# Input weights loaded in one piece per gate, and the weight sums of the head shared out anew (GRU with residual, one core)

## The chip, the cores and the metric

The kernel runs on one core of a Trainium2 chip. The metric is the device time of one execution in microseconds (us). Engines are named as in the profile: PE is TensorE (PEld its weight loads), DVE is VectorE, ACT is ScalarE, POOL is GpSimd, SP is SyncE, which here only issues DMAs.

## The reference

A GRU with 64 sequences, 128 steps and 512 features, all fp32; the output is the input plus the new state of every step. After each fourth step, except the last, the state goes through one more layer ("prop").

```python
comb  = concat([x_t, h])
z     = sigmoid(comb @ Wz + bz)
r     = sigmoid(comb @ Wr + br)
cand  = tanh(concat([x_t, r * h]) @ Wh + bh)
h_new = (1 - z) * h + z * cand
h     = tanh(h_new @ Wp + bp) if (t + 1) % 4 == 0 and t < T - 1 else h_new
out[:, t] = x_t + h_new
```

Wz, Wr and Wh have 1024 rows: the upper 512 meet x_t, the lower 512 meet the state.

## The kernel before

**Layout.** A tile has 128 partitions in four quarters of 32. The batch is split into two halves of 32 sequences, h = 0 and 1, and features into four blocks of 128. A half's rows stand on partitions by feature block. The state has to be turned for the products (features on partitions): VectorE does this in 32 x 32 blocks (`turn`, L238, for the state; `join_x`, L251, for x). Gates are called R, Z and H_ in the code; H is the candidate's gate.

**Two kinds of products.** The *hidden* part of each gate (state times the lower weights `wh`, and `wp` for prop) is the recurrence: `gate` (L218) adds it into the PSUM banks `rec[0]`, `rec[1]` (gates R, H and prop of half 0 and half 1) and `rec_z`. The *input* part (x times the upper weights `wx`) doesn't depend on the state, and is worked out ahead of need. For steps 0 to 3 it is done plainly (`plain`, L413); VectorE adds the bias and writes a tile `cp` (`add_bias`, L417). From step 4 on it is done in batches of four steps (`batch`) with a scheme of seven products in place of eight, on two levels, after Strassen and Winograd. It needs sums and differences of weights, made once in the head: on the outer level `tw` (six of 128 x 768, `sum_outer`, L286) and `d5` (two of 128 x 768, `sum_outer_1`, L292), on the inner level `tt` and `din` (`sum_inner` and `sum_inner_1`, L296 to L302: for each of seven operands i four of 128 x 384; operand 5 needs d5, operands 4, 6 and 7 need tw). It also needs sums of the turned x (`four`, L306; `sum_raw12`, `sum_raw34`, `sum_s12` and so on), which GpSimd makes. GpSimd also adds the bias (`with_bias`, L549) and puts the products together into `cp` (`add`, L544; `pair_left` and `pair_right` for the first batch of steps 4 to 7).

**Seeds.** Ahead of a gate, ScalarE copies the input part with bias from `cp` into the PSUM bank (`seed`, L376 to L379), and TensorE adds the hidden part onto it. Each engine takes its instructions in the order in which the program writes them. A gate in a bank `rec[h]` waits for every earlier write to this bank, also where the seed is for another gate's half of it.

**The order of a step.** `half(h)` (L781) is a generator that runs all steps of one half of the batch; two of them are interleaved, the second 700 columns behind the first. A step is gate R, gate Z, gate H, and prop after each fourth step; between them `fill` takes input products from a queue, as many as the tables PLACES, HEAD and TAIL say. Second half only: `behind_r`, `join` and `behind_step` write the GpSimd sums, the turns of x and the DMAs of the step. Seeds of step t+1 are written as soon as a bank is free; gate R's seed of step 4 is written in step 3, behind gate Z (L818 to L820), since `cp` of step 4 is late.

**The head.** Loads: x of steps 0 and 1 (`xr`), then the input weights of R, Z and H, with `load_w` (L98), each in four DMAs of 32 partitions (R in two halves of four), two of them on SyncE's queue and two on ScalarE's. Feature q\*128 + 32k + e of x lies on partition 32q + e in block k of `wx`, and join_x turns x to match. GpSimd's own DMA queue brings the biases and the first state. Then `later_loads` (L144): hidden weights, further x, Wp and the bias of prop. In the program stand next: two turns of x of steps 0 and 1, `later_loads`, the turn of the first state, the sums for operands 1 and 2 on VectorE, d5 and the sums for 3 and 5 on GpSimd, the plain products of steps 0 and 1 on TensorE with cp behind them, the seeds of step 0, and the steps.

Of the kernel before, what the change touches and what calls it, by code (L numbers as in the profile page):

```python
# [9 lines left out]
F32 = mybir.dt.float32  # L10
# [8 lines left out]
def kernel(  # L19
# [14 lines left out]
    nc = tc.nc  # L34
# [3 lines left out]
    S = 2  # L38
# [52 lines left out]
    def load_x(tile_, t0, n, j=0, engs=(nc.sync, nc.sync)):  # L91
        for h in range(S):
            for q in (0, 2, 1, 3):
                engs[q // 2].dma_start(
                    out=tile_[part(q), j : j + n, h, :], in_=x[ts(h, V), t0 : t0 + n, ts(q, J)]
                )

    def load_w(wt, w, k0=0, k1=K, engs=(nc.sync, nc.sync)):  # L98
        for q in (0, 2, 1, 3):
            engs[q // 2].dma_start(  # L100
                out=wt[part(q), k0:k1, :],
                in_=w[q * P + k0 * V : q * P + k1 * V, :].rearrange("(k e) n -> e k n", e=V),
            )

    both_queues = (nc.sync, nc.scalar)

    xr = {}
# [7 lines left out]
    new_xr(0)  # L115
    load_x(xr[0], 0, 2, engs=both_queues)
    for k in range(0, K, 2):
        load_w(wx[:, :, R, :], gates_in[R][:D], k, k + 2, both_queues)
    for i in (Z, H_):
        load_w(wx[:, :, i, :], gates_in[i][:D], engs=both_queues)  # L120

    for i, b in enumerate((br, bh, bz)):
        nc.gpsimd.dma_start(out=bias_row[:, i, :], in_=b.rearrange("(o n) -> o n", o=1))
# [3 lines left out]
    for h in range(S):  # L127
# [1 line left out]
            out=h_init[:, h, :],  # L129
            in_=h0[ts(h, V), :].rearrange("b (q j) -> q b j", q=NQ),  # L130
        )
    load_x(xr[0], 2, 2, 2)

    dummy = const.tile([1, 1], F32, name="dummy")
    nc.scalar.activation(dummy, ones[:, 0:1], AF.Sigmoid)
# [3 lines left out]
    def load_xs(g):  # L139
        if g * Q4 < T:  # L140
            xs[g] = one.tile([P, Q4, S, J], F32, tag=f"xs{g % 2}", name=f"xs_{g}")
            load_x(xs[g], g * Q4, Q4)

    def later_loads():  # L144
        for i in range(3):
            load_w(wh[i], gates_in[i][D:], engs=both_queues)
        new_xr(1)
        load_x(xr[1], Q4, Q4)
        load_xs(2)
        load_w(wp, Wp)  # L150
        for q in range(NQ):
            nc.sync.dma_start(
                out=bias_p[part(q)],
                in_=bp.rearrange("(o d c j) -> c o d j", o=1, d=2, c=2)[q % 2].broadcast_to(
                    [V, S, J]
                ),
            )
# [87 lines left out]
    def join_x(g, i):  # L245
        if g * Q4 >= T:
            return
        if g not in xT:
            xT[g] = xtp.tile([P, Q4, C, P], F32, tag="xT", name=f"xT_{g}")
        src = xr[g] if g < FIRST else xs[g]  # L250
        nc.vector.transpose(  # L251
            out=xT[g][:, i].rearrange("p c (a h b) -> p h (c a) b", a=S, h=S),
            in_=src[:, i].rearrange("p h (k e) -> p h k e", k=K),
        )

    def outer(kb, nb, ka):
        return wx[:, kb * S + ka, :, :].rearrange("p g (q n u) -> p n q g u", q=NQ, n=C)[:, nb]
# [27 lines left out]

    def sum_outer():  # L286
        for ka in range(S):
            nc.vector.tensor_sub(tw[3][:, ka], outer(1, 1, ka), outer(0, 1, ka))
            nc.vector.tensor_add(tw[2][:, ka], tw[3][:, ka], outer(0, 0, ka))
            nc.vector.tensor_sub(tw[4][:, ka], outer(1, 0, ka), tw[2][:, ka])  # L290

    def sum_outer_1(eng):  # L292
        for ka in range(S):
            eng.tensor_sub(d5[:, ka], outer(0, 1, ka), outer(0, 0, ka))
# [6 lines left out]
    def sum_inner_1(i, eng):  # L301
        eng.tensor_sub(leftover(i), inner(i, 0, 1), inner(i, 0, 0))  # L302
# [310 lines left out]
    for i in (1, 2):  # L613
        sum_inner(i, nc.vector)
        sum_inner_1(i, nc.vector)
    sum_outer_1(nc.gpsimd)
    for i in (3, 5):
        sum_inner(i, nc.gpsimd)
        sum_inner_1(i, nc.gpsimd)
# [53 lines left out]
    def behind_r(t, duo, u):  # L673
        odd = FIRST + 2 * duo + 1
        if t == 1:
            sum_inner(7, nc.gpsimd)
            sum_inner_1(7, nc.gpsimd)
        if t == 2:
            pair_left(0, 1, 2)
        elif t == 3:  # L680
            pair_right(0, 1, 10)
        if t == 4:
            sum_inner(4, nc.gpsimd)
            sum_inner_1(4, nc.gpsimd)
        if u == 0 and duo >= 1 and odd - 2 < LAST:
            outer_u2(odd - 2)

    def join(t, duo, u, n):
        even, odd = FIRST + 2 * duo, FIRST + 2 * duo + 1
        if t == 0:  # L690
            join_x(0, 2 + n)
        elif t == 1:
            join_x(1, 2 + n)
        elif t == 2:
            join_x(2, n)
        elif t == 4:
            join_x(3, 2 * n)
            join_x(3, 2 * n + 1)
        elif duo >= 0 and u in (5, 6):
            join_x(even + 2, 2 * (u - 5) + n)  # L700
        elif duo >= 1 and u in (1, 3):
            join_x(odd, u - 1 + n)

    def behind_step(t, duo, u, h_new):
        g, j = divmod(t, Q4)
        even, odd = FIRST + 2 * duo, FIRST + 2 * duo + 1
        if t == T - 8:
            pair_left(0, 1, 2, LAST)
        elif t == T - 6:
            pair_right(0, 1, 10, LAST)  # L710
        if t == 3:
            pair_left(1, 8, 9)
            pair_right(1, 8, 11)

        if duo >= 0:
            if u == 0 and duo >= 1 and odd - 2 < LAST:
                outer_c22(odd - 2)
                outer_c21(odd - 2)
            if even * Q4 < T:
                if u == 0:  # L720
                    sum_s34(even)
                elif u == 1:
                    outer_1(even)
                    outer_c11(even)
                    sum_raw12(odd)
                elif u == 2:
                    outer_u1(even)
                    outer_5(even)
                    sum_raw4(even)
                elif u == 3:  # L730
                    outer_c12(even)
                    outer_u2(even)
                    outer_c22(even)
                    if odd < LAST:
                        sum_s12(odd)
                elif u == 4:
                    if odd < LAST:
                        sum_s34(odd)
                    outer_c21(even)
                    if odd < LAST:  # L740
                        outer_1(odd)
                elif u == 5 and odd < LAST:
                    sum_raw4(odd)
                elif u == 6 and odd < LAST:
                    outer_u1(odd)
                    outer_c11(odd)
                elif u == 7 and odd < LAST:
                    outer_5(odd)
                    outer_c12(odd)
        if duo >= -1 and (even + 2) * Q4 < T:  # L750
            if t == 2 or (u == 6 and duo >= 0):
                sum_raw12(even + 2)
            if u == 7:
                sum_s12(even + 2)
        if t < T - 1:
            nc.gpsimd.tensor_add(xr[g][:, j], xr[g][:, j], h_new)  # L756

        n = 0
        if t >= T - CHUNK:
            n = 3 if t == T - 2 else 0  # L760
        elif j == Q4 - 1:
            n = 4
        if n:
            for h in range(S):
                for q in range(NQ):
                    nc.sync.dma_start(
                        out=out[ts(h, V), t - n + 1 : t + 1, ts(q, J)],
                        in_=xr[g][part(q), j - n + 1 : j + 1, h, :],
                    )
        if j == 1 and g >= 1 and (g + 1) * Q4 < T:  # L770
            new_xr(g + 1)
            load_x(xr[g + 1], (g + 1) * Q4, Q4)
        if t in (1, 2):
            load_xs(t + 2)
        if duo >= 0:
            if u == 3:
                load_xs(odd + 2)
            elif u == 6:
                load_xs(even + 4)

    def half(h):  # L781

        for t in range(T):
# [25 lines left out]
            if h == 1:  # L809
                for i in range(S):  # L810
                    crossed(z[:, i, :], i, Z, AF.Sigmoid)
                nc.vector.scalar_tensor_tensor(  # L812
                    out=keep, in0=z, scalar=1.0, in1=h_old, op0=ALU.subtract, op1=ALU.mult
                )
                join(t, duo, u, 1)
                if t == 1:
                    sum_raw34(1)
                if t == 3:  # L818
                    for i in range(S):
                        seed(R, t + 1, i)  # L820
                if last:
                    nc.gpsimd.tensor_sub(xr[g][:, j], xr[g][:, j], keep)
                if t == 0:
                    sum_outer()
                    join_x(1, 0)
                    join_x(1, 1)
                    sum_raw12(1)
                    sum_inner(6, nc.gpsimd)
                    sum_inner_1(6, nc.gpsimd)
                if t == 2:  # L830
                    for n in range(2, 4):
                        join_x(2, n)
# [21 lines left out]
                seed(H_, t + 1, h)  # L854
            if h == 1 and t != T - 2:
                seed(Z, t + 1, 0)
            if h == 1 and t == T - 5:
                for i in range(S):
                    seed(R, t + 1, i)
            state[t + 1] = h_new, hT  # L860
# [69 lines left out]
```

## Time and profile before

| what | us |
|---|---|
| median of three runs | 1290.0 (1289.52 to 1290.32) |
| the profiled execution | 1288.07 |
| its span | 1286.2 |
| granted TensorE clock, mean over the span | 0.993 |

The span is what the profile covers, from the first to the last instruction; 1.9 us of the profiled execution lie outside it. Times on the timeline count from the start of the span. A row of the timeline gives the start, the duration, the engine, the line and operation, the tiles written and read, their shape, and, in brackets, how long the engine was idle ahead of it and what ended that.

### The profile page before, as it was taken

The numbers are of one execution on the slowest core, as the hardware profiler recorded it, in microseconds if no ns is written. First come the engines' busy times: TensorE is split into PE (matmuls) and PEld (weight loads), VectorE is DVE, ScalarE is ACT, GpSimd is POOL, SyncE is SP. The second block draws the span as 40 slices with busy tenths as digits, with TensorE's granted clock in tenths as the row PEclk, the third lists the DMA queues.
The fourth block names the chain that finished last, engine by engine and source line by source line (L and its number), as shares of the span: only waits on it lengthen the run. The fifth ranks groups of instructions, "written<-read, shape, count | busy, mean of one in ns | idle before, by whom it ended". The sixth has DMA issues, their size and how long they took to land.

```text
span 1286.2 us, 60724 instructions
## 1 busy us (share of the span) xinstructions
PE 1253.8 (97%) x25968; PEld 1167.4 (91%) x25968; DVE 781.3 (61%) x2166; ACT 835.5 (65%) x2688; POOL 886.1 (69%) x1027
## 2 busy tenths in 40 slices
PE   6989999999999999999999999999999999999988
PEld 2679999999999999999999999999999999999766
DVE  4646666656665666666666666666656666666544
ACT  1446666666666666666766667666676666666655
POOL 5449777777677776777787677776777787677430
PEclk9989999999999999999999999999999999999999
DMA  8302211111121111111111121111112112111100
GB/s 224 82 19 52 52 36 41 47 36 52 40 61 39 29 45 51 52 36 53 38 34 52 46 58 36 33 45 45 52 36 57 38 28 52 52 35 36 26 25 21
DMA packets 113365, 60.82 MB, mean 47 GB/s; under 512 B 12969, under 2 KB 109481, under 8 KB 113097
## 3 DMA queue, kind: packets, MB, share of 16 engines
q1 hardware_dynamic: 110628, 53.46, 16.1%
q8 instruction: 205, 3.36, 1.1%
q10 hardware_dynamic: 2212, 3.34, 1.0%
q14 instruction: 64, 0.52, 0.1%
q0 software_dynamic: 256, 0.14, 0.1%
HBM read 40.11 MB, written 16.78 MB: 44 GB/s over the span
## 4 chain that ended last, share of the span: by engine, by line
PE 93%; DMA 2%; POOL 1%; issue 1%; ACT 1%; DVE 1%; SPq 0%; ACTq 0%; POOLq 0%; DVEq 0%
PE rec L209 42%; PE rec_z L209 15%; PE scratch_r L209 13%; PE scratch_q L209 10%; PE scratch_a L209 5%; PE scratch_x L209 4%; PE scratch_y L209 4%; DMA wx<-in_L_cond_Wh_dram 1%; DMA wh<-in_L_cond_Wh_dram 1%; DMA wh<-in_L_cond_Wr_dram 0%; POOL cp L544 0%; DMA wx<-in_L_cond_Wr_dram 0%; ACT rec_z L235 0%; POOL mb L549 0%; DVE rec_z L840 0%
## 5 line engine op out<-in xcount | busy, mean ns | idle before, releaser
L209 PE MATMUL rec<-wh,rhT 128*32 128x256 f32 x4096 | 377.1, 381 | 4.5 <-ACT rec L379 4.5
L209 PE MATMUL rec<-wh,hT 128*32 128x256 f32 x3072 | 281.3, 379 | 0.3 <-DVE hT L238 0.3
L209 PE MATMUL rec_z<-wh,hT 128*32 128x256 f32 x3072 | 281.3, 379 | 0.1
L209 PEld LDWEIGHTS rec<-wh,rhT 128*32 128x32 f32 x4096 | 251.2, 110 | 23.6 <-ACT rec L379 4.9
L379 ACT COPY rec<-cp 64x256 f32<-64x256 f32 x512 | 189.8, 371 | 42.6 <-DVE cp L417 17.0
L235 ACT ACTIVATE scratch_r<-rec 64x128 f32<-64x128 f32 x512 | 128.0, 250 | 134.0 <-PE rec L209 70.7
L209 PEld LDWEIGHTS rec_z<-wh,hT 128*32 128x32 f32 x3072 | 193.3, 110 | 7.1 <-ACT rec_z L379 0.6
L209 PEld LDWEIGHTS rec<-wh,hT 128*32 128x32 f32 x3072 | 187.2, 110 | 12.9 <-ACT c L235 1.5
L235 ACT ACTIVATE rec_z<-rec_z 64x128 f32<-64x128 f32 x512 | 128.0, 250 | 96.1 <-PE rec_z L209 84.0
L235 ACT ACTIVATE c<-rec 64x128 f32<-64x128 f32 x512 | 138.9, 271 | 64.2 <-PE rec L209 52.9
L756 POOL TENSOR_TENSOR xr<-xr,h 128x256 f32<-128x256 f32 x127 | 93.0, 732 | 88.0 <-DVE h L849 79.8
L544 POOL TENSOR_TENSOR mb<-mb,mb 128x768 f32<-128x768 f32 x58 | 106.2, 1831 | 67.1 <-DVE mb L512 67.0
L544 POOL TENSOR_TENSOR cp<-mb,mb 128x768 f32<-128x768 f32 x75 | 137.1, 1828 | 7.3 <-DVE mb L512 3.7
L544 POOL TENSOR_TENSOR cp<-mb 128x768 f32<-128x768 f32 x47 | 86.1, 1832 | 56.9 <-ACT rec_z L379 55.4
L812 DVE SCALAR_TENSOR_TENSOR keep<-rec_z,h 128x256 f32<-128x256 f32 x96 | 40.7, 424 | 133.8 <-ACT rec_z L235 128.6
L209 PE MATMUL scratch_r<-tw,s 128*32 128x192 f32 x928 | 120.9, 326 | 0.0
L485 ACT COPY cq<-scratch_q 128x384 f32<-128x384 f32 (+1 forms) x214 | 102.4, 478 | 19.5 <-PE scratch_q L209 18.0
L502 DVE TENSOR_TENSOR cx<-scratch_r,cx 128x384 f32<-128x384 f32 (+1 forms) x107 | 59.2, 554 | 86.5 <-PE scratch_r L209 76.6
L549 POOL TENSOR_TENSOR mb<-mb,bias_x 128x768 f32<-128x768 f32 x35 | 64.0, 1829 | 58.2 <-DVE mb L512 58.2
L209 PE MATMUL scratch_q<-tt,s 128*32 128x192 f32 x928 | 103.7, 326 | 0.0
L508 DVE TENSOR_TENSOR mb<-scratch_q,cx 128x384 f32<-128x384 f32 (+1 forms) x107 | 59.2, 553 | 58.5 <-ACT cq L485 58.4
L798 DVE TENSOR_TENSOR rh<-scratch_r,h 128x128 f32<-128x128 f32 x192 | 56.0, 291 | 63.3 <-ACT scratch_r L235 63.3
(182 smaller groups left out, 3844.6 us busy)
## 6 DMA issues: line engine op xcount, KB each, us to landing
out_dram<-xr SPq DMA_DIRECT2D x249, 64.0 KB, 1.8
xr<-in_x_dram SPq DMA_DIRECT2D x248, 64.0 KB, 2.2
xs<-in_x_dram SPq DMA_DIRECT2D x240, 64.0 KB, 2.2
wp<-in_L_cond_Wp_dram SPq DMA_DIRECT2D x4, 256.0 KB, 5.6
wx<-in_L_cond_Wr_dram SPq DMA_DIRECT2D x4, 128.0 KB, 2.7
wx<-in_L_cond_Wr_dram ACTq DMA_DIRECT2D x4, 128.0 KB, 2.8
wx<-in_L_cond_Wz_dram SPq DMA_DIRECT2D x2, 256.0 KB, 6.6
wx<-in_L_cond_Wz_dram ACTq DMA_DIRECT2D x2, 256.0 KB, 6.7
```

The lines of the kernel that those rows point to most:

```text
L209: nc.tensor.matmul(ps[part(2 * h + c)], lhsT=left, rhs=rhs(c), start=start, stop=True, skip_group_check=True,)
L235: nc.scalar.activation(dst[ts(d, 2 * V)], gate_ps(i, h)[ts(h, 2 * V), d, :], func)
L379: nc.scalar.copy(gate_ps(i, h)[rows].rearrange("p d (c n) -> p d c n", c=C), G[t][rows, :, :, i, :].rearrange("p c d n -> p d c n"),)
L485: nc.scalar.copy(c[:, :nm], ps[:, :nm])
L502: nc.vector.tensor_add(T2[what][:, :nm], r_ps[:, :nm], T2[what][:, :nm])
L508: nc.vector.tensor_add(blocks(1, 1), runs(q_ps[:, :nm]), runs(T2[what][:, :nm]))
L544: nc.gpsimd.tensor_add(dst, a, b)
L549: nc.gpsimd.tensor_add(m, m, v.unsqueeze(1).to_broadcast([P, 2, 3 * J]))
L756: nc.gpsimd.tensor_add(xr[g][:, j], xr[g][:, j], h_new)
L798: nc.vector.tensor_mul(rh[:, h, :], r_, h_old[:, h, :])
L812: nc.vector.scalar_tensor_tensor(out=keep, in0=z, scalar=1.0, in1=h_old, op0=ALU.subtract, op1=ALU.mult)
```

## The change

- The input weights are loaded by `load_wx`: one DMA over all 128 partitions for Z and for H, and two for R, all on SyncE's queue. Partition p holds the features 4p + k (k = 0 to 3), which are neighbouring rows of the weights in DRAM.
- `join_x` reads each fourth column of x, to match: four fp32, or 16 bytes, from one element to the next.
- x of steps 2 and 3 comes over GpSimd's DMA queue in place of SyncE's.
- `later_loads` begins with a copy of one element of Z's input weights on ScalarE (`held_2`), so that ScalarE's loads behind it are issued once Z has landed.
- d5 moves from GpSimd to VectorE, behind the sums for operands 1 and 2.
- `sum_outer` (tw) moves from VectorE, behind gate Z of step 0, to GpSimd, to the end of step 0, behind the four turns of x of group 1 (steps 4 to 7), which now all stand there, and `sum_raw12(1)` and `sum_raw34(1)`. The sums for operand 6 move to step 1, ahead of those for 7.
- Gate R's seed of step 4 moves from behind gate Z of step 3 to the end of gate H of half 1.

The order of TensorE's instructions is the same in both kernels.

```diff
+    def load_wx(i, k0=0, k1=K):
+        nc.sync.dma_start(
+            out=wx[:, k0:k1, i, :],
+            in_=gates_in[i][:D].rearrange("(p k) n -> p k n", k=K)[:, k0:k1],
+        )
...
     for k in range(0, K, 2):
-        load_w(wx[:, :, R, :], gates_in[R][:D], k, k + 2, both_queues)
+        load_wx(R, k, k + 2)
     for i in (Z, H_):
-        load_w(wx[:, :, i, :], gates_in[i][:D], engs=both_queues)
+        load_wx(i)
...
-    load_x(xr[0], 2, 2, 2)
+    load_x(xr[0], 2, 2, 2, (nc.gpsimd, nc.gpsimd))
...
+    held_2 = const.tile([1, 1], F32, name="held_2")
+
     def later_loads():
+        nc.scalar.copy(held_2, wx[0:1, 0, Z, 0:1])
...
         nc.vector.transpose(
             out=xT[g][:, i].rearrange("p c (a h b) -> p h (c a) b", a=S, h=S),
-            in_=src[:, i].rearrange("p h (k e) -> p h k e", k=K),
+            in_=src[:, i].rearrange("p h (e k) -> p h k e", k=K),
         )
...
     def sum_outer():
         for ka in range(S):
-            nc.vector.tensor_sub(tw[3][:, ka], outer(1, 1, ka), outer(0, 1, ka))
-            nc.vector.tensor_add(tw[2][:, ka], tw[3][:, ka], outer(0, 0, ka))
-            nc.vector.tensor_sub(tw[4][:, ka], outer(1, 0, ka), tw[2][:, ka])
+            nc.gpsimd.tensor_sub(tw[3][:, ka], outer(1, 1, ka), outer(0, 1, ka))
+            nc.gpsimd.tensor_add(tw[2][:, ka], tw[3][:, ka], outer(0, 0, ka))
+            nc.gpsimd.tensor_sub(tw[4][:, ka], outer(1, 0, ka), tw[2][:, ka])
...
-    sum_outer_1(nc.gpsimd)
+    sum_outer_1(nc.vector)
...
         if t == 1:
-            sum_inner(7, nc.gpsimd)
-            sum_inner_1(7, nc.gpsimd)
+            for i in (6, 7):
+                sum_inner(i, nc.gpsimd)
+                sum_inner_1(i, nc.gpsimd)
...
-        elif t == 1:
-            join_x(1, 2 + n)
...
-        if t == 3:
+        if t == 0:
+            for i in range(Q4):
+                join_x(1, i)
+            sum_raw12(1)
+            sum_raw34(1)
+            sum_outer()
+        elif t == 3:
             pair_left(1, 8, 9)
...
-                if t == 1:
-                    sum_raw34(1)
-                if t == 3:
-                    for i in range(S):
-                        seed(R, t + 1, i)
...
-                if t == 0:
-                    sum_outer()
-                    join_x(1, 0)
-                    join_x(1, 1)
-                    sum_raw12(1)
-                    sum_inner(6, nc.gpsimd)
-                    sum_inner_1(6, nc.gpsimd)
...
-            if h == 1 and t == T - 5:
+            if h == 1 and t in (3, T - 5):
                 for i in range(S):
                     seed(R, t + 1, i)
```

## The prediction

> **What bounds the kernel now.** I read the page's first and fourth parts, then TensorE's idle times on the timeline. Below: busy times with their share of the span, and the chain that ended last.
>
> ```profile
> span 1286.2 us, 60724 instructions
> PE 1253.8 (97%) x25968; PEld 1167.4 (91%) x25968; DVE 781.3 (61%) x2166; ACT 835.5 (65%) x2688; POOL 886.1 (69%) x1027
> PE 93%; DMA 2%; POOL 1%; issue 1%; ACT 1%; DVE 1%; SPq 0%; ACTq 0%; POOLq 0%; DVEq 0%
> ```
>
> TensorE is the bound; 32.4 us of the span are not its own. The change gives it no other products and leaves their order alone, so it can act only where TensorE waits, or by making a new wait. The large waits all stand in the first 90 us (timeline of TensorE: start, duration, instruction, in brackets the idle time ahead of it):
>
> ```profile
> 14.13 1.93 PE L209 MATMUL scratch_q<-wx,xT 128*32 128x256 f32 x32 [2.29 <-DMA wx<-in_L_cond_Wz_dram]
> 30.69 3.35 PE L209 MATMUL rec<-wh,hT_init 128*32 128x256 f32 x28 [9.26 <-DMA wh<-in_L_cond_Wh_dram]
> 83.67 0.64 PE L209 MATMUL rec<-wh,rhT 128*32 128x256 f32 x2 [4.50 <-ACT rec L379]
> 89.60 0.38 PE L209 MATMUL rec<-wp,hT 128*32 128x256 f32 x2
> ```
>
> So three questions: when step 0's first gate starts (30.69 now), what becomes of the stall in step 3 (4.50 us), and what each turn of x costs once it reads each fourth column. The span is one execution's, of 1288.07 us, 1.9 more than the span; that execution lies 1.9 below the median of the runs, 1290.0. I sum against 1288.07 and add 1.9 at the end.
>
> **Part 1, the head.** The releaser named at 30.69 is not the last one. VectorE's rows show what is:
>
> ```profile
> 17.74 0.56 DVE L297 TENSOR_TENSOR tt<-wx 128x384 f32<-128x384 f32 x1 [2.75 <-DMA xr<-in_x_dram]
> 18.34 2.07 DVE L298 TENSOR_TENSOR tt<-tt,wx 128x384 f32<-128x384 f32 x1
> 25.12 1.16 DVE L298 TENSOR_TENSOR tt<-tt,wx 128x384 f32<-128x384 f32 x1
> 28.72 0.74 DVE L417 TENSOR_TENSOR cp<-scratch_q,bias_x 128x256 f32<-128x256 f32 x2
> ```
> ```profile
> 17.78 4.30 POOL L294 TENSOR_TENSOR d<-wx 128x768 f32<-128x768 f32 x2 [4.55 <-DMA xr<-in_x_dram]
> ```
> ```profile
> 29.17 0.77 ACT L379 COPY rec<-cp 64x256 f32<-64x256 f32 x2 [17.01 <-DVE cp L417]
> ```
>
> The last input weights (H) land just ahead of 17.74. Then VectorE does eight sums until 28.72, each slowed by GpSimd's sums beside it (2.07 and 1.16 against 0.56 alone); only then come cp, ScalarE's copy into the bank, and TensorE 1.97 us after 28.72. So H's landing plus 12.95 is TensorE's start.
>
> After the change VectorE also takes d5 (two sums of 768), while GpSimd keeps only the sums for 3 and 5, and those for 5 wait for d5. Prices without a neighbour, on VectorE and GpSimd:
>
> ```profile
> 39.77 0.92 DVE L288 TENSOR_TENSOR tw<-wx 128x768 f32<-128x768 f32 x1
> ```
> ```profile
> 48.06 1.01 POOL L297 TENSOR_TENSOR tt<-tw 128x384 f32<-128x384 f32 x1
> ```
>
> GpSimd's four sums for 3 cover some four of VectorE's, which run at the pitch of the rows 25.12 and after (about 1.27); the rest run alone: 0.6 + 4 x 1.27 + 3 x 0.58 + 2 x 0.97 = 9.35, plus 1.97: landing plus 11.3, a gain of 1.6 at equal landing.
>
> The landing itself moves. Windows (busy of PE, PEld, DVE, ACT, POOL, then granted clock, DMA share, GB/s):
>
> ```profile
> 4.00:16.00 12.00, 9.71 (x148) 4.43 (x144) 1.39 (x4) 2.41 (x5) 2.51 (x4) 1.00 0.98 275
> 8.00:10.00 2.00, 2.00 (x44) 1.13 (x40) 0.00 (x0) 0.28 (x1) 0.00 (x0) 1.00 1.07 321
> 38.00:42.00 4.00, 4.00 (x80) 2.38 (x76) 2.87 (x5) 0.94 (x4) 0.00 (x0) 1.00 0.97 242
> ```
>
> The DMA engines are full already, so one DMA instead of four can only change the rate. Ahead of Z's landing go x 0.26, R 1.05, Z 1.05 and some 0.2 MB of h0 and x rows; about 0.3 MB are through by 4 us. At a rate r (MB per us) Z lands at 4 + 2.26/r. There held_2 releases ScalarE's hidden weights; I estimate 1.3 us until they flow, then they share the engines with H half and half. The rest of H at half rate and 0.2 MB more of small loads give H's landing at 2.7 + 4.56/r: 19.3 by 0.275, 21.5 by 0.242 (SP's queue alone, the nearest row for a single queue, but of x and Wp rows of 32 partitions), 16.9 by 0.321. Without the sharing it would be 4 + 3.51/r, 14.9 by 0.321. I take 0.321, since each load now addresses all 128 rows and the window of 8 to 10 shows the engines can do it; hence 16.9 + 11.3 = 28.2, **a gain of 2.5** (from +4.5 to -2.1). The hidden weights of R, 1.05 MB, half of it behind H, are in by about 20.5, ahead of need. The x rows 2 and 3 and h0 on POOL's queue are needed only in steps 0 to 3, so they cost nothing. The clock after the pause is as before, also half speed for one stretch:
>
> ```profile
> 26.80:33.60 6.80, 2.91 (x24) 1.33 (x28) 3.99 (x8) 1.79 (x5) 4.72 (x5) 0.50 0.97 205
> 81.50:88.20 6.70, 4.53 (x50) 3.54 (x54) 1.24 (x3) 2.45 (x7) 1.71 (x1) 0.50 0.01 2
> ```
>
> **Part 2, step 3.** Today ScalarE's queue stops at the seed R of step 4, which waits for GpSimd's cp; behind it stands what gate H of step 3 needs. That is the 4.50 us, and the second window above shows half clock behind it (4.53 busy at half rate, some 2.3 us lost). The move of that seed behind gate H takes the stall from 79.17 away: what TensorE does from 83.67 to 89.60 in 5.9 us takes 3.65 at full clock, so it would reach the prop gate at 82.8. But now the prop gate waits, since the seed R is written to its bank ahead of it, and stands on ScalarE behind seed Z, which waits for the same cp. So when is GpSimd there? Its rows now (the sums tw are VectorE's there):
>
> ```profile
> 50.27 0.41 DVE L417 TENSOR_TENSOR cp<-scratch_x,bias_x 128x256 f32<-128x256 f32 x1
> ```
> ```profile
> 46.28 0.46 POOL L310 TENSOR_TENSOR s12r<-xT 128x128 f32<-128x128 f32 x1 [14.60 <-DVE xT L251]
> 52.18 0.72 POOL L756 TENSOR_TENSOR xr<-xr,h 128x256 f32<-128x256 f32 x1
> 61.64 1.83 POOL L549 TENSOR_TENSOR mb<-mb,bias_x 128x768 f32<-128x768 f32 x1 [1.71 <-DVE mb L512]
> 63.55 1.83 POOL L544 TENSOR_TENSOR cp<-mb 128x768 f32<-128x768 f32 x1
> 73.65 0.46 POOL L310 TENSOR_TENSOR s12r<-xT 128x128 f32<-128x128 f32 x1 [8.27 <-PE scratch_r L209]
> 79.53 1.80 POOL L549 TENSOR_TENSOR mb<-mb,bias_x 128x768 f32<-128x768 f32 x1
> 81.41 1.80 POOL L544 TENSOR_TENSOR cp<-mb,mb 128x768 f32<-128x768 f32 x1
> ```
>
> GpSimd was idle for 8.27 and 1.71 us in this stretch; the added work is more than that. On the clock of before: the last two turns of group 1 stand behind cp (50.68) and end at 51.5; s12r and s34r, 2 x 1.8, to 55.1; six sums tw at the price of a 768 (1.83, pitch 1.88), 11.3, to 66.4; xr 0.7; sums 6 and 7, 2 x 4.1 (48.06 to 52.18), to 75.3; xr 0.7; mb and cp 3.7, to 79.7; then the stretch 73.65 to 79.53 (5.9), to 85.6; mb and cp 3.7: **89.3** against 83.2 now. Seeds Z and R, 0.38 each, and TensorE starts the prop gate at 90.1, +0.5 against 89.60. The pause before it is 7.3 us, longer than the 4.50, so I expect half clock again behind it; by the two windows that costs 0 to 3.3 us, and I take 1.6. GpSimd's later work has no new debt. Step 3 thus costs **+2.1**. Were GpSimd's six sums slower (2.15, as the two at 17.78), it would be 2 more.
>
> Smaller: TensorE first uses s12r here, and needs the third of its four sums:
>
> ```profile
> 53.02 0.33 PE L209 MATMUL scratch_x<-tt,s12r 128*32 128x192 f32 x2
> ```
>
> The third sum ends at about 51.5 + 3 x 0.48 = 52.96: nothing, or up to 0.5 us if the turns are slower. Behind held_2 on ScalarE stand its hidden loads, counted above, and the seeds, which come long after Z's landing; so its wait costs nothing else.
>
> **Part 3, x turned by each fourth column.** 128 turns read with a stride of 16 bytes. No row of before does this. Lower bound of the extra: 0. Upper: from the slope of the two sizes of turn (all turns of x in one group row: least, median, most; then VectorE, then TensorE):
>
> ```profile
> L251 DVE STREAM_TRANSPOSE xT<-xs x120: 401/434/449, 63.4 to 1195.8; 128x256 f32<-128x256 f32 x120
> 448.23 0.43 DVE L251 STREAM_TRANSPOSE xT<-xs 128x256 f32<-128x256 f32 x1
> 448.59 0.27 DVE L840 TENSOR_TENSOR rec_z<-c,rec_z 128x128 f32<-128x128 f32 x1
> 449.28 0.31 DVE L238 STREAM_TRANSPOSE hT<-h 128x128 f32<-128x128 f32 x1
> ```
> ```profile
> 449.84 0.41 PE L209 MATMUL rec<-wh,hT 128*32 128x256 f32 x2
> ```
>
> 0.43 - 0.31 over 128 elements is 0.94 ns each; half rate would add 0.24 us to a turn. Most turns lie in VectorE's idle 39%. Two in each eight steps (like 448.23) stand with no gap ahead of L840, whose line to hT's turn (ends 449.59) and TensorE (449.84) is the recurrence; there the slack is 0.25, some 0.15 of it is signalling, so about 0.25 us is lost per eight steps, 15 times 3.7, with 0.7 in the head. The extra is 0 to 4.4. I take 0, the nearest row being the same turn at 0.434 of the same elements. [...]
>
> **Sum.** -2.5 + 0.5 + 1.6 + 0 = -0.4 on 1288.07: 1287.7; on the median, **1289.6**.
>
> **The rivals.**
> A, the forecast: about 1289.6, chance 0.47; with it the case that the loads are no faster and the change of layout buys nothing (0.275, H at 19.3: +2.4, 1292.0).
> B, slower: the strided turn runs at half rate, +4.4, 1294.0. It decides as soon as a turn of x is over some 0.5 us, beyond the slack of 0.25 less signalling. For it: those places with no gap; against: 0.434 so far, where the write side is spread and shows no price. Chance 0.27.
> C, faster: loads over 128 rows are so quick that H lands at 14.9 or earlier, as without sharing (2 us more; up to 3.5 more if r is higher), so 1287.5 to 1286; for it: the 321; against: DMA share 0.98 already. Chance 0.2.
> D, faster: GpSimd does the six tw at VectorE's price (0.92). That saves 5.5 in its sum, the cp ends by 83.8, the pause is short and step 3 gains some 3 instead of costing 2.1: 1284.5. Against: each of GpSimd's rows of 768. Chance 0.06.
>
> **How the numbers follow.** Range: from the fast end of C and most of the way to D, 1285.0, to B with loads no faster (1296.4), rounded down to 1296.0. A measurement of this kernel tells about 0.2% (2.6 us) from no change: faster is below 1287.4, slower above 1292.6. Faster: D and most of C, 0.24; slower: B and a little of A, 0.3; same: 0.46.
>
> **What would show it.** H's landing by VectorE's first sum (16.9), TensorE's first hidden product (28.2), no idle ahead of the first rec<-wh,rhT of step 3, an idle of about 7 us ahead of the first rec<-wp,hT, GpSimd's six tw at 1.83, and the turn of x at 0.43 (A) or 0.67 (B). It is wrong if there is a wait outside the first 95 us, or if the clock after the prop gate's pause isn't at half.

## The result, and the profile after

The changed kernel takes 1293.03 us (median of 13 runs, 1291.31 to 1295.45), the kernel before 1289.85 in the same 13 rounds (1288.31 to 1290.75): a ratio of 1.0027, 95% interval 1.0018 to 1.0036. It is **slower by 3.2 us**, a quarter of a per cent. The forecast was 1289.6, no change; 1293.03 lies in the range, but on the side of rival B (1294.0).

The profiled execution took 1291.31 us, the shortest of the 13; like the one of before (1288.07) it lies 1.7 to 1.8 below its median, so the two can be set side by side. Its busy times and the chain that ended last:

```profile
span 1289.5 us, 60714 instructions
PE 1260.4 (98%) x25968; PEld 1144.8 (89%) x25968; DVE 799.6 (62%) x2162; ACT 835.6 (65%) x2689; POOL 897.2 (70%) x1039
PE 91%; POOL 4%; DVE 2%; issue 1%; ACT 1%; DMA 1%; POOLq 0%; DVEq 0%; ACTq 0%
```

TensorE is still the bound, but GpSimd has gone from 1% to 4% of the chain. VectorE has 18 us more to do with as many operations. TensorE's large idle times on the timeline, to set beside the four of before:

```profile
27.38 3.58 PE L218 MATMUL rec<-wh,hT_init 128*32 128x256 f32 x28 [4.96 <-ACT rec L388]
50.50 0.36 PE L218 MATMUL scratch_x<-tt,s12r 128*32 128x192 f32 x2 [0.18 <-POOL s12r L321]
87.44 0.64 PE L218 MATMUL rec<-wp,hT 128*32 128x256 f32 x2 [6.98 <-ACT rec L388]
```

Step 0 starts 3.31 us earlier (30.69 before); the 4.50 us ahead of gate H of step 3 have gone; ahead of the prop gate of step 3 stand 6.98 us that weren't there. But this row starts at 87.44, still 2.16 earlier than its counterpart (89.60), so the loss comes behind it. Since TensorE's order is the same, each of its instructions has a counterpart. First an instruction of step 4, then one near the end, in the kernel before:

```profile
103.66 0.38 PE L209 MATMUL rec<-wh,hT 128*32 128x256 f32 x2
1259.09 0.41 PE L209 MATMUL rec<-wh,hT 128*32 128x256 f32 x2
```

and after:

```profile
103.94 0.41 PE L218 MATMUL rec<-wh,hT 128*32 128x256 f32 x2
1262.07 0.41 PE L218 MATMUL rec<-wh,hT 128*32 128x256 f32 x2
```

At 103.66 the changed kernel is 0.28 behind, at 1259.09 it is 2.98 behind. So the difference of these two executions splits up like this (after minus before, all from counterparts):

| stretch | us | predicted |
|---|---|---|
| head, to the middle of step 0 | -2.86 | -2.5 |
| wait for s12r at 50.5 | +0.4 | 0 |
| start of the prop gate of step 3 | +0.3 | +0.5 |
| half clock behind that pause | +2.4 | +1.6 |
| the 1155 us that follow | +2.7 | 0 |
| sum | +3.0 | -0.4 |

The remaining 0.3 of the spans' 3.3 lie behind TensorE's last products. The head's share holds for this pair alone: when the weights land differs from execution to execution (with the loads of the changed kernel VectorE's first sum behind H starts at 16.34 to 18.61, see below).

**The head.** VectorE's rows after:

```profile
16.34 0.56 DVE L306 TENSOR_TENSOR tt<-wx 128x384 f32<-128x384 f32 x1 [2.09 <-DMA xr<-in_x_dram]
16.93 1.25 DVE L307 TENSOR_TENSOR tt<-tt,wx 128x384 f32<-128x384 f32 x1
22.14 0.56 DVE L307 TENSOR_TENSOR tt<-tt,wx 128x384 f32<-128x384 f32 x1
23.68 1.82 DVE L303 TENSOR_TENSOR d<-wx 128x768 f32<-128x768 f32 x2
25.41 0.75 DVE L426 TENSOR_TENSOR cp<-scratch_q,bias_x 128x256 f32<-128x256 f32 x2
```

The same sum takes 1.25 beside GpSimd and 0.56 alone; both d5 take 1.82. From the first sum to TensorE 11.04 us (12.95 before).

**Step 3.** GpSimd's first and last tw, and the cp that all wait for; then ScalarE's seeds, Z first and R behind it:

```profile
52.61 1.84 POOL L297 TENSOR_TENSOR tw<-wx 128x768 f32<-128x768 f32 x1
62.06 1.84 POOL L299 TENSOR_TENSOR tw<-wx,tw 128x768 f32<-128x768 f32 x1
84.88 1.80 POOL L553 TENSOR_TENSOR cp<-mb,mb 128x768 f32<-128x768 f32 x1
```
```profile
86.71 0.38 ACT L388 COPY rec_z<-cp 128x256 f32<-128x256 f32 x1 [6.22 <-POOL cp L553]
87.02 0.76 ACT L388 COPY rec<-cp 64x256 f32<-64x256 f32 x2
```

And the pause with its clock (windows; the column behind the five engines is the granted clock):

```profile
80.00:84.00 4.00, 0.46 (x12) 0.08 (x2) 0.95 (x4) 0.46 (x2) 3.84 (x7) 1.00 0.00 0
84.00:88.00 4.00, 0.56 (x8) 0.43 (x12) 0.00 (x0) 1.05 (x3) 2.60 (x2) 0.69 0.00 0
88.00:92.00 4.00, 4.00 (x48) 3.14 (x44) 1.80 (x4) 1.26 (x4) 1.27 (x1) 0.50 0.00 0
92.00:96.00 4.00, 4.00 (x92) 3.31 (x86) 0.91 (x4) 2.00 (x6) 3.92 (x3) 0.96 0.02 4
```

TensorE is idle through two windows, and the clock falls while it is; from 88 to 92 it is busy all the time, at half clock (48 products where the next window has 92).

**The turns of x.** All turns in one group, then the place that the prediction looked at, on VectorE and on TensorE:

```profile
L260 DVE STREAM_TRANSPOSE xT<-xs x120: 618/664/699, 61.0 to 1198.6; 128x256 f32<-128x256 f32 x120
449.19 0.67 DVE L260 STREAM_TRANSPOSE xT<-xs 128x256 f32<-128x256 f32 x1
449.77 0.27 DVE L842 TENSOR_TENSOR rec_z<-c,rec_z 128x128 f32<-128x128 f32 x1
450.54 0.31 DVE L247 STREAM_TRANSPOSE hT<-h 128x128 f32<-128x128 f32 x1
```
```profile
451.00 0.41 PE L218 MATMUL rec<-wh,hT 128*32 128x256 f32 x2
```

0.664 us in place of 0.434: as by the upper bound, which took half rate (0.67). The counterparts show where it is lost. The lag of the changed kernel grows in steps, each behind a place where a turn of x stands directly ahead of the candidate's product, and by next to nothing between. At 411 it is 0.98, at 450 (the place above) 1.16. The next two, before and then after:

```profile
488.02 0.41 PE L209 MATMUL rec<-wh,hT 128*32 128x256 f32 x2
526.72 0.41 PE L209 MATMUL rec<-wh,hT 128*32 128x256 f32 x2
```
```profile
489.24 0.41 PE L218 MATMUL rec<-wh,hT 128*32 128x256 f32 x2
528.05 0.41 PE L218 MATMUL rec<-wh,hT 128*32 128x256 f32 x2
```

So the lag is 1.22 at 488 and 1.33 at 527. Steps of about 0.06 and 0.11 alternate over nearly the whole run; the 0.18 at 450 is the largest. Eight steps together lose some 0.18.

### The profile page after: what moved, and what is told of

It is laid out like the page before. It is cut to its first block, busy times and chain, and to the rows that moved or that the text cites. A ratio compares the mean times of both kernels' runs of the same rounds, so it can differ in the third digit from the quotient of the medians.

```text
span 1289.5 us, 60714 instructions
## 1 busy us (share of the span) xinstructions
PE 1260.4 (98%) x25968; PEld 1144.8 (89%) x25968; DVE 799.6 (62%) x2162; ACT 835.6 (65%) x2689; POOL 897.2 (70%) x1039
## 4 chain that ended last, share of the span: by engine, by line
PE 91%; POOL 4%; DVE 2%; issue 1%; ACT 1%; DMA 1%; POOLq 0%; DVEq 0%; ACTq 0%
PE rec L218 41%; PE rec_z L218 15%; PE scratch_r L218 13%; PE scratch_q L218 10%; PE scratch_a L218 5%; PE scratch_x L218 3%; PE scratch_y L218 3%; DMA xr<-in_x_dram 1%; POOL cp L553 1%; POOL mb L558 0%; ACT rec_z L244 0%; DMA wx<-in_L_cond_Wr_dram 0%; POOL tw L298 0%; POOL tw L297 0%; POOL xr L770 0%
## 5 line engine op out<-in xcount | busy, mean ns | idle before, releaser
L218 PE MATMUL rec<-wh,rhT 128*32 128x256 f32 x4096 | 373.1, 379 | 0.0
L218 PEld LDWEIGHTS rec<-wh,rhT 128*32 128x32 f32 x4096 | 239.3, 110 | 23.6 <-ACT scratch_r L244 1.8
L218 PEld LDWEIGHTS rec<-wh,hT 128*32 128x32 f32 x3072 | 172.9, 110 | 22.4 <-ACT rec L388 6.3
L218 PEld LDWEIGHTS rec_z<-wh,hT 128*32 128x32 f32 x3072 | 182.4, 110 | 8.7 <-ACT rec_z L388 0.6
L218 PE MATMUL scratch_r<-tw,s 128*32 128x192 f32 x928 | 118.0, 326 | 0.0
L218 PE MATMUL rec<-wp,hT 128*32 128x256 f32 x992 | 92.9, 387 | 8.6 <-ACT rec L388 8.6
```

What stands on the lines that cost most here:

```text
L218: nc.tensor.matmul(ps[part(2 * h + c)], lhsT=left, rhs=rhs(c), start=start, stop=True, skip_group_check=True,)
```

## The experiments

The theory: the changed kernel's +3.2 are a gain in the head (about -2.9), a loss in step 3 (+2.8), because GpSimd's tw make its cp late, and a loss of some 3 us by the strided turn of x, through two places in each eight steps. The rivals: the slow drift has another cause; the seed's move itself is what costs in step 3.

**The stride alone.** On the kernel before:

```diff
+    def load_wx(i, k0=0, k1=K, engs=(nc.sync, nc.sync)):
+        for q in (0, 2, 1, 3):
+            engs[q // 2].dma_start(
+                out=wx[part(q), k0:k1, i, :],
+                in_=gates_in[i][q * P : (q + 1) * P, :].rearrange("(e k) n -> e k n", k=K)[:, k0:k1],
+            )
...
-            in_=src[:, i].rearrange("p h (k e) -> p h k e", k=K),
+            in_=src[:, i].rearrange("p h (e k) -> p h k e", k=K),
```

> The kernel before with the layout alone changed: input weights still in four loads of 32 partitions on both queues, but feature 4p+k on partition p, and x turned by each fourth column. Theory (the strided turn costs 0.66 us in place of 0.43, and TensorE loses some 0.25 us in each eight steps behind the two turns that stand directly ahead of the candidate's product on VectorE): mean turn 0.66, TensorE falls behind the kernel before by 0.07 and 0.18 us alternately, 2.7 us over the whole run, and 0.2 in the head: ratio 1.0022, about 1292.8. Rival (the drift of the changed kernel comes from elsewhere, such as GpSimd's or the DMAs' work, and the longer turns lie in idle time): turn 0.66, ratio 1.000.

Measured: 1293.28 (before 1289.54), ratio 1.0031, interval 1.0019 to 1.0042. The group of its turns, and the two counterparts of above:

```profile
L258 DVE STREAM_TRANSPOSE xT<-xs x120: 607/664/681, 66.5 to 1201.8; 128x256 f32<-128x256 f32 x120
```
```profile
107.27 0.41 PE L216 MATMUL rec<-wh,hT 128*32 128x256 f32 x2
1265.30 0.41 PE L216 MATMUL rec<-wh,hT 128*32 128x256 f32 x2
```

1158.03 us between the two, 1155.43 before: +2.60. The turn and the drift are as the theory has them. The rest of this execution's difference arose earlier: its weights landed 1.95 later (VectorE's first sum starts at 19.69), 1.1 more arose in step 0, where two products of gate Z at 36.07 still take 0.64 us (0.38 at their counterpart, 33.87), and 0.5 from there to step 4.

**The stride halved.** As the run above, with each second column of two groups and the loads of Z and H split to match:

```diff
...
-            out=xT[g][:, i].rearrange("p c (a h b) -> p h (c a) b", a=S, h=S),
-            in_=src[:, i].rearrange("p h (k e) -> p h k e", k=K),
+            out=xT[g][:, i].rearrange("p c (a h b) -> p h c a b", a=S, h=S),
+            in_=src[:, i].rearrange("p h (j e b) -> p h j b e", j=2, b=2),
```

> As the stride alone, but x is turned by each second column (8 bytes from one element to the next, feature 64j+2e+b of each block), so two elements of a turn lie in each 16 bytes; the weights' loads of Z and H are split in two to match. [...]

Measured: 1287.93, ratio 0.9988 (0.9979 to 0.9997).

```profile
L259 DVE STREAM_TRANSPOSE xT<-xs x120: 401/436/461, 62.0 to 1194.4; 128x256 f32<-128x256 f32 x120
```

No price at 8 bytes (0.436, against 0.434 in the kernel before), all of it at 16 (0.664 in the run above), and the lag between the two counterparts grows by 0.05 only. The 1.6 us that it is quicker had not been expected. In its profile step 0 starts 1.26 us earlier than before: 0.76 because H lands earlier, and 0.5 because GpSimd's d5 starts 2.2 us behind VectorE's first sums, two of which then run at 0.56.

**The old layout in the changed kernel.** x turned from neighbouring columns, four DMAs per gate over 128 partitions:

```diff
+        for k in range(k0, k1):
+            nc.sync.dma_start(
+                out=wx[:, k, i, :],
+                in_=gates_in[i][:D].rearrange("(q k e) n -> k q e n", q=NQ, e=V)[k],
+            )
...
-            in_=src[:, i].rearrange("p h (e k) -> p h k e", k=K),
+            in_=src[:, i].rearrange("p h (k e) -> p h k e", k=K),
```

> The changed kernel with the old layout of features and x turned from neighbouring columns; the weights are loaded over 128 partitions on SyncE's queue still, one DMA per block k (four per gate, 2 KB rows). Theory: turn 0.43, no drift, the wait for s12r goes, so 3.1 less than the changed kernel: 1289.9, ratio 1.000, if H lands at 16.3 as there. Rival on the loads (one load per gate with 8 KB per partition is what made H land early): H lands at 17.7 or later and a third of the head's gain goes, about 1291.2. Rival on the drift (not the turn): 1293.

Measured: 1315.94, ratio 1.0204. The turns are back at 0.435, and against the kernel before the lag grows by 0.15 from 103.66 to 1087 us on the clock of before (by 2.25 in the changed kernel); 0.4 more arise behind that, from a cause that isn't shown. But the head takes 27 us more. The window of the loads, there and in the changed kernel:

```profile
4.00:16.00 12.00, 9.49 (x96) 2.85 (x88) 0.77 (x2) 1.08 (x4) 4.74 (x9) 0.70 0.33 109
```
```profile
4.00:16.00 12.00, 12.00 (x124) 4.34 (x120) 1.77 (x4) 1.35 (x5) 6.83 (x12) 1.00 1.03 314
```

The DMA engines are busy a third of the time (a share of 0.33, against 1.03). The pattern in DRAM is 4 quarters of 32 rows in place of 128 rows at one pitch; what leaves the engines idle isn't shown. The run says nothing on the loads' part in the gain.

**Two turns moved.** In the changed kernel, the turns directly ahead of the candidate's product after a prop gate go behind the turn of the state:

```diff
-            join_x(even + 2, 2 * (u - 5) + n)
+            if (u, n) != (5, 1):
+                join_x(even + 2, 2 * (u - 5) + n)
...
-            join_x(odd, u - 1 + n)
+            if (u, n) != (1, 1):
+                join_x(odd, u - 1 + n)
...
+        if duo >= 0 and u == 5:
+            join_x(even + 2, 1)
+        elif duo >= 1 and u == 1:
+            join_x(odd, 1)
```

> The changed kernel with two of each eight steps' turns moved behind the step's turn of the state on VectorE: those that stand directly ahead of the candidate's product after a prop gate (the other turns stay, all stay strided). Theory: turn still 0.66, but no drift: 2.7 less than the changed kernel, 1290.3, ratio 1.0004. Rival (the longer turns cost at other places too, or something else makes the drift): 1293, or part of it.

Measured: 1291.04, ratio 1.0011 (1.0002 to 1.0020), 2.0 less than the changed kernel. The turn is still 0.664, and the lag between the two counterparts grows by 0.26 in place of 2.70. So it is the place that makes the price count.

**tw back on VectorE**, in the changed kernel, behind gate Z of step 0 (`sum_outer` with `nc.vector`, called where it was):

> The changed kernel with the six sums tw back on VectorE, behind gate Z of step 0 as before; all else as changed. Theory (step 3 pays because GpSimd's 11.3 us of tw make its cp 6 us late, and the prop gate waits 7 us for it, with the clock at half behind the pause): cp ends at about 80.8 on the changed kernel's clock, TensorE waits about 1 us ahead of the prop gate in place of 6.98, no half clock behind it; 8 us less than the changed kernel: 1285, ratio 0.996. Rival 1 (the time lost in step 3 is the seed's move, not tw): cp still late, 1293. Rival 2 (VectorE's 5.7 us of tw stop step 0, now that all four turns of the next group stand in it): an idle time of 1 to 3 us by 45 to 50, 1287.

Measured: 1284.78, ratio 0.9965 (0.9953 to 0.9978). The prop gate of step 3:

```profile
84.10 0.41 PE L218 MATMUL rec<-wp,hT 128*32 128x256 f32 x2 [1.10 <-ACT rec L388]
```

1.10 us in place of 6.98, full clock behind it (1.00 granted from 84 to 96 us), 8 us less in all. Neither rival holds.

**The seed back** behind gate Z of step 3, in the changed kernel:

> The changed kernel with gate R's seed of step 4 back behind gate Z of step 3; all else as changed. Theory (the seed's place only decides which gate of step 3 waits for GpSimd's cp, which ends at about 86.7): TensorE waits some 10.4 us ahead of gate H of step 3 and not at all ahead of the prop gate, half clock through gate H: 3 us slower than the changed kernel, 1296, ratio 1.005. Rival (the move of the seed is itself what costs): 1290.

Measured: 1296.18, ratio 1.0053 (1.0040 to 1.0065).

```profile
89.68 0.64 PE L218 MATMUL rec<-wh,rhT 128*32 128x256 f32 x2 [10.31 <-ACT rec L388]
```

The move of the seed is worth 3 us even with the late cp.

**ScalarE's hidden weights held until H**, in the changed kernel (`held_2` copies from `wx[0:1, 0, H_, 0:1]`):

> The changed kernel with ScalarE's hidden weights held until H's input weights land, not Z's. Theory (they share the DMA engines with H half and half from Z's landing on): H lands some 2 us earlier, at 14 to 15, TensorE starts step 0 some 2 us earlier, and the hidden weights are still in time: 1291, ratio 1.001. Rival (the loads of x and the state and SyncE's queue set H's landing): H as in the changed kernel, 1293. Rival (hidden weights of gate R come late then): TensorE waits for them past the seeds, 1293 to 1295.

Measured: 1293.76, ratio 1.0032 (1.0021 to 1.0042). A miss. VectorE's first sum, and two windows:

```profile
20.67 0.56 DVE L306 TENSOR_TENSOR tt<-wx 128x384 f32<-128x384 f32 x1 [4.36 <-DMA wh<-in_L_cond_Wz_dram]
```
```profile
8.00:10.00 2.00, 2.00 (x44) 1.08 (x36) 0.00 (x0) 0.00 (x0) 2.00 (x4) 1.00 1.05 410
16.00:20.00 4.00, 0.00 (x0) 0.00 (x0) 0.31 (x1) 0.00 (x0) 1.54 (x2) 0.73 1.01 190
```

H landed later, at about 20.6 (TensorE's first product with it starts at 20.68, behind a wait of 6.20 us for its load), though ScalarE's hidden weights stand behind the copy that waits for it. 410 GB/s were moved from 8 to 10 us, and 190 from 16 to 20, with the DMA engines about as busy (1.05 and 1.01). So ScalarE's share is not needed for a late landing, and holding it back gained nothing in the median.

**x of steps 2 and 3 on SyncE's queue again**, in the changed kernel (`load_x(xr[0], 2, 2, 2)`):

> The changed kernel with x of steps 2 and 3 on SyncE's queue again, behind the input weights. After the miss of the run that held ScalarE's hidden weights until H: theory (from 10 us on GpSimd's queue, with its small pieces of x and of the state, slows the one queue that carries H): H lands at 14.5 to 15.5, 1.5 less: 1291.5, ratio 1.0012. Rival (it is SyncE's own hidden weights behind H, or the shape of the loads): H at 16 to 18.5 as in the changed kernel, 1293, ratio 1.0027.

Measured: 1292.52, ratio 1.0024 (1.0015 to 1.0034). H landed at about 16.6 (TensorE's first product with it starts at 16.68, behind a wait of 1.47 us for its load) and step 0 started at 27.67: the rival's number. So x on GpSimd's queue isn't the cause either. But the rival's reason isn't shown by this run: SyncE's own hidden weights stand behind the rows of x on its queue here. The run above shows that ScalarE's hidden weights aren't needed for a late landing; for SyncE's it isn't shown.

**Both repairs.** tw on VectorE and the two turns moved:

> The changed kernel with both: tw back on VectorE behind gate Z of step 0, and the two turns of each eight steps behind the turn of the state. Theory (the two costs are separate and add): turns still 0.66, no drift (2.7 less), and no long wait in step 3 (8 less): 1282.5 to 1283, ratio 0.9945. Rival (they overlap, or VectorE's tw costs in the head): 1285 to 1287.

Measured: 1282.99, ratio 0.9951 (0.9938 to 0.9963). The two add: 8.2 and 2.0 by themselves, 10.0 together.

**d5 alone**, on the kernel before (`sum_outer_1(nc.vector)`):

> The kernel before with one part of the change: d5 on VectorE, behind the sums for 1 and 2. Theory (VectorE's sums are slow only beside GpSimd's): from the first sum to TensorE's start of step 0 11.0 us in place of 12.95: 1.9 less, 1287.9, ratio 0.9985. Rival (GpSimd's sums for 3 and 5, now later, come late for step 2 or hold cp): 1290 or more.

Measured: 1286.91, ratio 0.9984 (0.9975 to 0.9993).

```profile
18.96 0.56 DVE L297 TENSOR_TENSOR tt<-wx 128x384 f32<-128x384 f32 x1 [5.12 <-DMA xr<-in_x_dram]
```
```profile
29.98 3.64 PE L209 MATMUL rec<-wh,hT_init 128*32 128x256 f32 x28 [6.22 <-ACT rec L379]
```

11.02 from the first sum to TensorE. H landed 1.2 later than in the profile of before, and yet TensorE starts earlier.

**The seed alone**, on the kernel before:

> The kernel before with one part of the change: gate R's seed of step 4 behind gate H of step 3. Theory (with tw on VectorE, GpSimd's cp ends at 83.2 and TensorE is ready for the prop gate at 82.8): no wait ahead of gate H, 1.2 us ahead of the prop gate, no half clock: 5.5 less, 1284.3, ratio 0.9957. Rival (the wait only moves to the prop gate, as in the changed kernel): 1289 to 1290.

Measured: 1283.66, ratio 0.9957 (0.9944 to 0.9969).

```profile
85.02 0.41 PE L209 MATMUL rec<-wp,hT 128*32 128x256 f32 x2 [1.18 <-ACT rec L379]
```

The gain is 6.0 us (5.5 by the ratio), and the wait is the 1.2 us that the theory had.

**d5, the seed and the pairs' layout**, on the kernel before:

> The kernel before with d5 on VectorE, gate R's seed of step 4 behind gate H of step 3, and the pairs' layout with its split loads (1.6 less by itself). Theory (the three are separate): 1.6 + 1.9 + 5.5 less: 1281, ratio 0.993, the quickest. Rival (the pairs' run was quicker for the same reason as d5, GpSimd starting later beside VectorE's first sums): 1282.5, ratio 0.9945.

Measured: 1282.56, ratio 0.9944 (0.9932 to 0.9957): the rival's number. It is no more of a gain than d5 and the seed make by themselves (2.7 and 6.0 by their medians, against 7.1 here; the difference is within the intervals), so the pairs' layout adds nothing that shows. In its profile 11.61 us lie between the first sum (17.61) and TensorE (29.22), more than the 11.02 with d5 alone. d5 and the seed without the pairs weren't tried together. It is the lowest median here, with that of both repairs in its interval.

## Why the prediction was wrong

**Part 3 is the step that failed: "I take 0, the nearest row being the same turn at 0.434".** The bounds were 0 and 4.4, and the upper one had the right size of the turn, 0.67 by half rate (0.664 measured), lost in two places of each eight steps. The 0.15 that it took off the slack as signalling is what the changed kernel shows between the end of the state's turn (450.85) and TensorE's product (451.00). As a sum the upper bound was too large by a third: 0.25 in each eight steps by the text, some 0.18 measured, and so 3.7 worked out against 2.7 over the run. But for the cost of a new access pattern the row of the same operation with the old pattern is no neighbour; its duration says only what the operation costs without the thing in question. Rival B, which was priced by the upper bound, should have had more than 0.27. The runs show 0.664 us for a turn with one fp32 in each 16 bytes, 0.436 with two and 0.434 with four. 2.7 us in place of 0 is most of the miss of 3.4 (+3.0 against -0.4). The estimate for the head (0.7) was too large: TensorE's wait for a turned x in step 0 grew by only 0.19 (1.04 to 1.23).

**Part 1 was right in its size, in part by luck.** The share of the sums came out (11.3 worked out; 11.04, and 11.02 with d5 alone), but not in every execution: with tw back on VectorE and with the seed back it was 12.13 and 12.16. There VectorE's first sum took 2.47 and 2.50 in place of 0.56, in a stretch (16 to 20 us) of which GpSimd was busy for 3.27 and 3.35 of the 4 us. H's landing, 16.9 worked out, was 16.2 in the profiled run; in four other runs with the same loads VectorE's first sum behind it starts at 17.02 to 18.61. But it was worked out with ScalarE's weights flowing 1.3 us after Z's landing and taking half of the DMA engines. The 1.3 us were the author's estimate, and no run shows them. Half is what each of the two queues had in the kernel before (0.37 MB on SyncE's and 0.38 MB on ScalarE's from 5 to 8 us). In the changed kernel ScalarE's weights were issued from 10.62 on, and of the 0.98 MB moved from 12 to 16 us 0.76 came by SyncE's queue, 0.18 by GpSimd's and 0.02 by ScalarE's. And the run that holds these weights back longer shows H later, not earlier. So that the number fits is luck. Rival C loses its ground with this: it drew on the same idea. What sets H's landing stays open; the rate of the loads of 32 partitions that are in flight with H wasn't tried by itself. The landing may also make part of the scatter of the run times, but with one trace of each kernel that isn't shown.

**Part 2 was right, with one term too small.** The wait ahead of the prop gate was worked out as 7.3 and was 6.98; the prop gate was to start 0.5 later and did by 0.3. The half clock behind the pause cost 2.4 where 1.6 stood, in the bounds of 0 to 3.3. What the prediction didn't weigh is that this part joins a large gain (the seed, 6.0 alone) to a larger loss (tw on GpSimd, 8), so it named step 3 as a small cost and not as the place where the change gives its gain away.

**Smaller:** the third sum of s12r came late (0 to 0.5 by the text, 0.4 measured), probably since the turns that it waits for are slower: with the old layout in the changed kernel TensorE doesn't wait there.

Rival B had the cause and the sign; D was excluded by GpSimd's rows as said (1.84 for the tw shown above).

So the change's parts, one at a time: the seed -6.0, d5 -2.7 (2.1 by its ratio), tw on GpSimd +8, the turn's stride +2.0 or more (what moving two of the turns gives back) and the loads about nothing that could be told from the landing's scatter. The tw and the turns were timed in the changed kernel, the other two in the kernel before. These numbers add to 1.3 or more of the 3.2; what the loads and the stride cost besides isn't separated.

## What to carry to other kernels

When a change alters how an operation reads its data, don't price it by a row with the old pattern. Bound it from both sides (half rate was the right upper bound for a turn here: 0.67 worked out, 0.664 measured) and look for the places where that operation stands right ahead of the recurrence: nearly all of the 2.7 us lost over 1155 us came from two places in each eight steps, and moving the turns there left 0.26. When work goes from a fast engine to a slow one that has idle time (a tw took 0.92 us on VectorE and 1.84 on GpSimd), add up the slow engine's queue until the next result that others wait for; six sums of 1.84 us on an engine with 10 us of slack cost 8 us, since the pause of 7 us also cost 2.4 us at half clock behind it. Split a change that moves several things, and time each: here two of its lines alone give 6.0 and 2.7 us, and the whole is slower.

## What the runs showed of the hardware that was not expected

- A turn of 128 x 256 fp32 took 0.436 us with 8 bytes from element to element, 0.434 with 4, and 0.664 with 16.
- The busy share of the DMA engines was no measure of their rate here: with ScalarE's hidden weights held until H they moved 410 GB/s at a share of 1.05 from 8 to 10 us, while the loads over 128 partitions were under way, and 190 GB/s at 1.01 from 16 to 20. Loads whose pattern in DRAM is four quarters of 32 rows left them busy at 0.33, with 109 GB/s, from 4 to 16 us; in the changed kernel it was 1.03, with 314.
- After the pause of 6.98 us the granted clock was 0.50 from 87.44 to about 92.3, some 5 us of work; with tw back on VectorE a pause of 1.10 us left it at 1.00.
- A sum of 128 x 384 fp32 on VectorE that takes 0.56 us alone took 1.2 to 2.5 us while GpSimd did sums: 1.25 in the changed kernel, 2.07 in the kernel before, 2.47 with tw back on VectorE.
